# A transformer block on one core: modulation sums in four column groups, square roots kept in written order, and loads moved between queues

## The chip, the cores and the metric

The kernel runs on one core of a Trainium2 chip. The metric is the device time of one execution in microseconds (us). Three executions of the kernel before took 2512.04 us in the median (2508.9 to 2512.86). Besides these there is one profiled execution, whose records all readings below come from.

The engines are named as in the profile: PE is TensorE (PEld its weight loads), DVE is VectorE, ACT is ScalarE, POOL is GpSimd, SP is SyncE, which here does nothing but issue transfers. ACT and POOL can issue transfers too.

## The reference

The input x has two sequences (B = 2) of T = 2048 tokens with D = 512 features; there is one condition vector of 512 values for each sequence. Everything is float32.

```python
mod = silu(condition) @ Wada + bada                    # 6 rows of 512 for each sequence
sh_a, sc_a, gt_a, sh_m, sc_m, gt_m = jnp.split(mod, 6, axis=1)
xm = layernorm(x, g1, be1) * (1.0 + sc_a) + sh_a
x = x + gt_a * attention(xm, Wqkv, Wproj, bproj)       # causal, 16 heads of 32
xm = layernorm(x, g2, be2) * (1.0 + sc_m) + sh_m
h = gelu(xm @ W1 + b1)                                  # 2048 hidden features
x = x + gt_m * (h @ W2 + b2)
```

## The kernel before

The kernel goes through five kinds of stage, the first three once for each sequence.

**Start.** Rows of small parameters (condition, g1, be1, g2, be2, b1) are loaded into the tile `rows` by ACT's queue, turned into columns by one transpose (`ps_c`, copied to `cols`), and silu of the condition goes into `sc`. `modulation(s0)` computes two of the six modulation rows at once: eight products of `sc` (128 rows, 32 columns) with 512 columns of `Wada`, which add up into two groups of 32 partitions of the bank `ps_mod`. DVE adds the bias rows (`mr` or `modr`, loaded from `bada` by ACT's queue), and, where the row is needed as columns, four transposes (`ps_modt`) and a copy follow. It runs three times: at the start, inside group 1 of the first sequence, and inside group 2.

**QKV** (class `Qkv`, L745 ff.). A sequence is cut into four groups (g = 0 to 3) of 512 tokens. `group(g)` makes eight chunks, n = 0 to 7, of queries and keys (`ps_qk`; four products each), then four of values (`ps_v`). Each chunk of queries or keys is split into a high and a low part in a tile `hl`, of which there are two: ACT writes the high half (L797), DVE the low half (L798), and SP stores the tile to memory (L803). The next chunk but one can be written only when that store has landed. After chunk 1, SP also issues the loads of the first keys and queries (`load_keys`, `load_queries`), which wait for the stores before them.

The layernorm of the *next* group is written inside the present one: `between(5)` calls `norm(g + 1, 0)`, and `between(8)` calls `norm(g + 1, 1)`. The first takes the statistics of four tiles of x on DVE, one square root for the four tiles on ACT and a reciprocal on DVE (`inv_std`, L207 to L209), scales the tiles on DVE (`xn`, L229), transposes two of them on PE (`ps_xt`, eight transposes), and applies scale and shift (`xmT`, L248 on DVE and L253 on ACT).

**Order.** A framework schedules the instructions of each engine and may move them against the order in which they are written, by a cost model of its own, except those that pass through `tc.keep_in_program_order`: all of PE's work (`mm`, `transpose`), and what is wrapped in `act(...)`. In the kernel before, the square root of `inv_std` and the copies `hl` are not wrapped, so the scheduler places them on ACT as it sees fit. Each engine then works through its own list from the front; a waiting instruction holds up those behind it.

**Attention** for all 16 heads, 16 units of work; its last act is to store the last unit's row sums (`sum`, L619).

**Projection** (`project_phase`, L913). 16 tiles of tokens, n = 0 to 15, each four products `ps_o`, to which DVE adds the residual (L968) and of which it takes statistics. POOL adds the bias row to the residual first (L961). DVE also multiplies the next quarter's attention output by the inverse row sums (L974). The last unit's sums come back in at n = 0 (`load_sums`, L949, the transfer `r<-sum`), are inverted at n = 3 (L329) and spread at n = 4. During the first sequence's projection the second sequence's QKV weights (`wqkv`, three transfers of 1 MB) are loaded, written at `between(6)`, on ACT's queue; its first layernorm runs at n = 5 and n = 8.

**MLP**, for both sequences together, with seven products in place of eight for each pair of blocks.

Of the kernel before, what the change touches and what calls it, by code (L numbers as in the profile page):

```python
# [8 lines left out]
F32 = mybir.dt.float32  # L9
# [18 lines left out]
def dit_block_kernel(  # L28
# [91 lines left out]
        nc.vector.memset(m.bitcast(F32), 0.0)  # L120
        mhl.append(m)

    pick = const.tile([2 * HD, B, P], F32, tag="pick", name="pick")
    for r in (0, HD):
        nc.vector.tensor_copy(
            pick[r : r + HD],
            ident[r : r + HD, r : r + B].unsqueeze(2).to_broadcast([HD, B, P]),
        )


    cols = const.tile([P, 64], F32, tag="cols", name="cols")
    mod = const.tile([P, 6, C, B], F32, tag="mod", name="mod")
    modr = const.tile([2 * HD, D], F32, tag="modr", name="modr")
    nc.gpsimd.memset(modr, 0.0)
    a1 = const.tile([P, C, B], F32, tag="a1", name="a1")
    c1 = const.tile([P, C, B], F32, tag="c1", name="c1")
# [9 lines left out]
    r_g1 = n_cond  # L146
    r_be1, r_g2, r_be2 = r_g1 + C, r_g1 + 2 * C, r_g1 + 3 * C
    r_b1 = r_g1 + 4 * C
    n_rows = r_b1 + FC


    qd = [
# [30 lines left out]
    def col(r, n):  # L183
        return cols[:, r : r + n]
# [5 lines left out]
    def mm(*args, **kw):  # L190

        return tc.keep_in_program_order(nc.tensor.matmul(*args, **kw))  # L192
# [5 lines left out]
    def transpose(dst, src):  # L198
        n = src.shape[0]
        return tc.keep_in_program_order(nc.tensor.transpose(dst, src, ident[:n, :n]))  # L200
# [4 lines left out]
        nc.vector.bn_aggr(mv[:, n, :], st)  # L205

    def inv_std(mv, rstd, lo, hi):  # L207
        nc.scalar.activation(rstd[:, lo:hi], mv[:, lo:hi, 1], AF.Sqrt, bias=eps)
        nc.vector.reciprocal(rstd[:, lo:hi], rstd[:, lo:hi])  # L209

    def rows_of(psum, r, b, tag):

        ps = psum.tile([P, D], F32, tag=tag, name="ps_rows")
        g = slice(r * HD, (r + 1) * HD)
        mm(ps, pick[g, b, :], modr[g, :], start=True, stop=True)
        return ps

    def transposed(pool_, psum, xts, n0, mv, rstd, a, c, b, dst):
# [523 lines left out]
    class Qkv:  # L742
# [15 lines left out]
        def load_w(self, queue):  # L758
            w_v = Wqkv.rearrange("(c p) f -> p c f", p=P)
            for f in range(0, 3 * D, D):  # L760
                queue.dma_start(self.w[:, :, f : f + D], w_v[:, :, f : f + D])

        def norm(self, g, j):

# [154 lines left out]
    def project_phase(row, psum, between):  # L919

        b = row.b
        with pool(f"proj{b}") as pp:
            n = 0
            ats = list(row.at_s)
            rbs = {1: row.rb_s[1], 2: row.old_queries(), 3: row.rb_s[0]}
            rows_x = [b * NT + i * TQ + t for i in last_order for t in range(TQ)]
            xts = list(row.xt_s)  # L930

            def tokens(upto):
                while len(xts) < min(upto, NT):
                    xt = pp.tile([P, D], F32, tag="xt", name="xt", bufs=6)
                    nc.sync.dma_start(xt, x_rows(rows_x[len(xts)]))
                    xts.append(xt)

            tokens(TQ + 6)
            for k, i in enumerate(last_order):
                if k in (0, 1):  # L940

                    at = pp.tile([P, C, QB], F32, tag="at", name="at", bufs=2)
                    nc.sync.dma_start(at, od[b][last_order[k + 2]])
                    ats.append(at)
                at = ats[k]
                for t in range(TQ):

                    if n == 0:
                        row.load_sums(len(units) - 1, len(units))  # L949
                        nc.sync.dma_start(rbs[2], wide_d[b][last_order[2]])  # L950
                        nc.sync.dma_start(
                            rbs[3][:, : C - 1], wide_d[b][last_order[3]][:, : C - 1]
                        )
                    elif n == 3:
                        row.invert(len(units) - 1, len(units))
                    elif n == 4:
                        row.widen(len(units) - 1, rbs[3][:, C - 1, :])

                    tokens(n + 6)
                    nt, xt = rows_x[n], xts[n]  # L960
                    act(nc.gpsimd.tensor_tensor(xt, xt, bgate, ALU.add))  # L961
                    ps = psum.tile([P, D], F32, tag="mm", name="ps_o")
                    for c in range(C):
                        mm(
                            ps, at[:, c, t * P : (t + 1) * P], row.wproj[:, c, :],
                            start=(c == 0), stop=(c == C - 1),
                        )
                    nc.vector.tensor_tensor(xt, ps, xt, ALU.add)  # L968
                    stats(pp, xt, nt, mv2)
                    nc.sync.dma_start(x1d[nt], xt)  # L970
                    if k + 1 < NQ:
                        d = ats[k + 1][:, t, :]
                        act(
                            nc.vector.tensor_tensor(d, d, rbs[k + 1][:, t, :], ALU.mult)  # L974
                        )
                    between(n)
                    n += 1
        inv_std(mv2, rstd2, b * NT, (b + 1) * NT)


    row = Row(0)
    with pool("wada") as wp, pool("qkv0") as qp, pool(
# [3 lines left out]
        for r, n, src in (  # L986
            (0, n_cond, cond.rearrange("b (c p) -> (b c) p", p=P)),
            (r_g1, C, g1.rearrange("(c p) -> c p", p=P)),
            (r_be1, C, be1.rearrange("(c p) -> c p", p=P)),
            (r_g2, C, g2.rearrange("(c p) -> c p", p=P)),  # L990
            (r_be2, C, be2.rearrange("(c p) -> c p", p=P)),
            (r_b1, FC, b1.rearrange("(c p) -> c p", p=P)),
        ):
            nc.scalar.dma_start(rows[r : r + n, :], src)
        wada_v = Wada.rearrange("(c p) f -> p c f", p=P)
# [2 lines left out]
        def load_wada(s0, s1):  # L998
            w = wp.tile([P, 2, C, D], F32, tag="wada", name="wada")
            if s0 % 3 == 2:  # L1000
                mr = modr
            else:
                mr = wp.tile([2 * HD, D], F32, tag="mr", name="mr")
                nc.gpsimd.memset(mr, 0.0)
            for n, s in enumerate((s0, s1)):
                nc.scalar.dma_start(
                    mr[n * HD : n * HD + B, :],
                    bada[s * D : (s + 1) * D].partition_broadcast(B),
                )
            for k in range(C):  # L1010
                for n, s in enumerate((s0, s1)):
                    nc.sync.dma_start(w[:, n, k, :], wada_v[:, k, s * D : (s + 1) * D])
            wada[s0] = w, mr
# [8 lines left out]
        nc.vector.tensor_copy(cols[:, :n_rows], ps_c)  # L1022
        sc = wp.tile([P, C, HD], F32, tag="sc", name="sc")
        nc.vector.memset(sc, 0.0)
        nc.scalar.activation(
            sc[:, :, :B], col(0, n_cond).rearrange("p (b c) -> p c b", c=C), AF.Silu
        )

        def modulation(s0):

            w, mr = wada.pop(s0)
            ps = ps_sp.tile([2 * HD, D], F32, tag="s", name="ps_mod")
            for k in range(C):
                for n in range(2):
                    mm(
                        ps[n * HD : (n + 1) * HD, :], sc[:, k, :], w[:, n, k, :],
                        start=(k == 0), stop=(k == C - 1),  # L1040
                    )
            nc.vector.tensor_tensor(mr, ps, mr, ALU.add)
            if s0 % 3 == 2:
                return
            ps_t = ps_sp.tile([P, C, 2 * HD], F32, tag="s", name="ps_modt")
            for k in range(C):
                transpose(ps_t[:, k, :], mr[:, k * P : (k + 1) * P])
            nc.vector.tensor_copy(
                mod[:, s0 : s0 + 2],
                ps_t.rearrange("p c (s r) -> p s c r", s=2)[:, :, :, :B],  # L1050
            )

        def scale_shift(a, c, r_g, r_be, shift, scale):

# [6 lines left out]
            nc.vector.tensor_tensor(c, c, mod[:, shift], ALU.add)  # L1061

        halves = [qkv.norm(0, j) for j in range(2)]
        modulation(0)
        scale_shift(a1, c1, r_g1, r_be1, 0, 1)
        for modulate in halves:
# [31 lines left out]
    with pool("qkv1") as qp, pool("ps_qkv1", bufs=6, space=PSUM) as ps_mm:  # L1098
# [2 lines left out]

        def between(n):
            if n == 6:
                qkv.load_w(nc.scalar)
            if n in (5, 8):
                qkv.norm(0, n // 8)()

# [21 lines left out]
    with ExitStack() as mlp:  # L1129
# [38 lines left out]
            return w  # L1168


        vec = wp.tile([B + 1, D], F32, tag="vec", name="vec")
        gb = wp.tile([P, C, B + 1], F32, tag="gb", name="gb")
        gbias = wp.tile([P, C, B], F32, tag="gbias", name="gbias")

        def gate_columns():
            ps = ps_op.tile([P, C, B + 1], F32, tag="o", name="ps_g")
            for k in range(C):
                transpose(ps[:, k, :], vec[:, k * P : (k + 1) * P])
            nc.vector.tensor_copy(gb, ps)
            nc.vector.tensor_tensor(  # L1180
                gbias, gb[:, :, :B], gb[:, :, B:].to_broadcast([P, C, B]), ALU.mult
            )

        def between(n):
            if n == 0:
                nc.vector.tensor_copy(vec[:B], modr[HD : HD + B])
                nc.sync.dma_start(vec[B:], b2.unsqueeze(0))
            if n == 4:
                gate_columns()
            if n in (5, 7):  # L1190
# [283 lines left out]
```

## Time and profile before

| | |
|---|---|
| time, median of 3 | 2512.04 us (2508.9 to 2512.86) |
| profiled execution, time | 2510.99 us |
| its span, first to last instruction | 2509.3 us |
| PE busy | 2440.3 us, 97% of the span |
| DVE busy | 1401.8 us, 56% |
| POOL busy | 978.7 us, 39% |
| ACT busy | 892.6 us, 36% |
| mean TensorE clock granted | 0.990 |

The profiled execution took 2510.99 us, of which 2509.3 us lie between its first and its last instruction. A row of the order in time reads: start in us, length in us, engine, line, operation, output<-input, sizes, count, and in brackets how long the engine sat idle before it and what it then waited for. A matrix product of float32 appears as two records, a transpose as one. "PEclk" in a table of stretches is the share of full clock that TensorE was granted.

### The profile page before, as it was taken

Reading aid. Unit: us, or ns where it says so; the run is one execution under the profiler, and the core shown is the slowest. Engines: PE = TensorE matmul, PEld = TensorE weight load, DVE = VectorE, ACT = ScalarE, POOL = GpSimd, SP = SyncE. Lnnn points to the kernel's source line nnn. Section 1 sums busy time; section 2 is a strip of 40 time slices with the busy share of each in tenths; the row PEclk is TensorE's granted clock in tenths of the full one; section 3 lists DMA queues with packets and bytes.
Section 4 is the critical chain, followed back from the end, with each engine's and each line's share of the span. In section 5 each row is a group of like instructions: output and inputs, shape, how many; then the busy total and the mean of one; then the engine's idle time right before and its main releaser. Section 6 shows DMA issues by size and latency. Waiting matters only on the chain.

```text
span 2509.3 us, 30950 instructions
## 1 busy us (share of the span) xinstructions
PE 2440.3 (97%) x10977; PEld 1178.9 (47%) x10977; DVE 1401.8 (56%) x2820; ACT 892.6 (36%) x1667; POOL 978.7 (39%) x1158
## 2 busy tenths in 40 slices
PE   7999999999999999999999999999999999999998
PEld 3445545445444444554554454444444444444443
DVE  3455667767666535567676766664363353344424
ACT  1213555554545012155545454613313312311310
POOL 0052786766762361068667675332101101200200
PEclk9999999999999999999999999999999999999999
DMA  6667123051224695440514113263224233332423
GB/s 223 202 218 202 46 50 87 22 110 43 87 88 144 215 302 193 133 95 22 110 43 110 27 51 118 69 226 114 88 92 140 78 101 109 109 96 70 140 84 96
DMA packets 133445, 285.71 MB, mean 114 GB/s; under 512 B 13301, under 2 KB 42525, under 8 KB 128426
## 3 DMA queue, kind: packets, MB, share of 16 engines
q1 hardware_dynamic: 126226, 257.47, 34.4%
q0 software_dynamic: 5376, 23.07, 2.6%
q10 hardware_dynamic: 1688, 3.19, 0.4%
q8 instruction: 86, 1.41, 0.2%
q14 instruction: 69, 0.57, 0.1%
HBM read 209.76 MB, written 81.79 MB: 116 GB/s over the span
## 4 chain that ended last, share of the span: by engine, by line
PE 62%; DVE 3%; DMA 1%; SPq 1%; issue 1%; ACT 0%; DVEq 0%; ACTq 0%
PE ps_h L192 15%; PE ps_y L192 15%; PE st L192 9%; PE o L192 5%; PE s L192 5%; PE ps_qk L192 4%; PE ps_o L192 3%; PE sm L192 2%; PE ps_v L192 2%; SPq L336 1%; PE ps_xt L200 1%; PE ps_o L200 0%; DMA r<-sum 0%; DMA q<-hl 0%; DVE junk L436 0%
## 5 line engine op out<-in xcount | busy, mean ns | idle before, releaser
L565 ACT ACTIVATE e<-st 128x512 f32<-128x512 f32 (+1 forms) x1152 | 572.8, 579 | 516.7 <-PE st L192 458.0
L441 DVE TENSOR_REDUCE mx<-s 128x1 f32<-128x512 f32 x634 | 429.6, 687 | 236.2 <-PE s L192 233.4
L593 POOL TENSOR_TENSOR ee<-e 128x512 f32<-128x512 f32 x336 | 420.2, 1287 | 242.8 <-ACT e L565 242.8
L192 PE MATMUL s<-kst,qst 128*128 128x512 f32 (+3 forms) x1066 | 483.4, 460 | 28.4 <-DVE mx L441 10.4
L192 PE MATMUL st<-qst,kst 128*128 128x512 f32 (+3 forms) x1280 | 405.3, 393 | 0.0
L192 PE MATMUL o<-e,vv 128*32 128x512 f32 (+3 forms) x2560 | 296.5, 545 | 0.0
L192 PEld LDWEIGHTS s<-kst,qst 128*128 128x128 f32 x1066 | 201.3, 190 | 202.3 <-DVE mx L441 80.4
L192 PE MATMUL ps_h<-sx,w 128*128 128x512 f32 x640 | 286.7, 592 | 0.0
L1245 POOL TENSOR_TENSOR c<-c 128x512 f32<-128x512 f32 x32 | 40.6, 1270 | 626.8 <-DVE c L1207 626.8
L436 DVE CUSTOM_DVE_ANT_0 junk<-s,causal 128x384 bf16<-128x384 f32 (+3 forms) x432 | 212.2, 491 | 126.9 <-PE s L192 118.2
L192 PE MATMUL ps_y<-sh,w 128*128 128x512 f32 x640 | 276.7, 592 | 0.0
L192 PEld LDWEIGHTS st<-qst,kst 128*128 128x128 f32 x1280 | 226.9, 193 | 92.8 <-issue 63.2
L192 PE MATMUL ps_qk<-xmT,wqkv 128*128 128x512 f32 x512 | 242.0, 601 | 2.2 <-DVE xmT L248 2.2
L571 POOL TENSOR_SCALAR_AFFINE_SELECT e<-e 128x128 f32<-128x128 f32 (+1 forms) x384 | 122.8, 344 | 290.2 <-ACT e L565 284.2
L1207 DVE TENSOR_TENSOR h<-c,ps_h 128x512 f32<-128x512 f32 x128 | 88.0, 688 | 232.5 <-PE ps_h L192 232.5
L593 POOL TENSOR_TENSOR ee<-ee 128x512 f32<-128x512 f32 x168 | 211.2, 1285 | 0.0
L192 PEld LDWEIGHTS ps_h<-sx,w 128*128 128x128 f32 x640 | 121.1, 190 | 150.2 <-issue 149.7
L192 PEld LDWEIGHTS ps_y<-sh,w 128*128 128x128 f32 x640 | 120.7, 190 | 147.8 <-issue 146.4
L1231 ACT ACTIVATE h<-h,cols 128x512 f32<-128x512 f32 x128 | 92.3, 721 | 182.4 <-DVE h L1207 182.4
L192 PE MATMUL st<-fold,sel 32*128 32x512 f32 (+1 forms) x1152 | 154.0, 485 | 2.3 <-DVE fold L500 2.0
L192 PEld LDWEIGHTS ps_qk<-xmT,wqkv 128*128 128x128 f32 x512 | 95.2, 192 | 98.7 <-issue 91.2
L192 PEld LDWEIGHTS st<-fold,sel 32*128 32x128 f32 x1152 | 61.2, 183 | 145.3 <-ACT e L565 75.2
(123 smaller groups left out, 2361.8 us busy)
## 6 DMA issues: line engine op xcount, KB each, us to landing
qst<-q SPq DMA_DIRECT2D x128, 256.0 KB
w<-w1d SPq DMA_DIRECT2D x34, 896.0 KB
w<-w2d SPq DMA_DIRECT2D x28, 1024.0 KB
kst<-k SPq DMA_DIRECT2D x24, 1024.0 KB
q<-hl SPq DMA_DIRECT2D x32, 512.0 KB
k<-hl SPq DMA_DIRECT2D x32, 512.0 KB
kst<-k SPq DMA_DIRECT2D x32, 256.0 KB
w<-in_L_cond_W_dram POOLq DMA_DIRECT2D x64, 128.0 KB, 4.3
```

The lines of the kernel that those rows point to most:

```text
L192: return tc.keep_in_program_order(nc.tensor.matmul(*args, **kw))
L200: return tc.keep_in_program_order(nc.tensor.transpose(dst, src, ident[:n, :n]))
L336: nc.sync.dma_start(dst, inv_d[self.b][u].unsqueeze(1).to_broadcast([HC, HD, QB]),)
L436: nc.vector.tensor_tensor_reduce(junk[:, :w], s[:, :w], causal[:, QB - w :], 1.0, MASKED, ALU.add, ALU.max, m,)
L441: nc.vector.tensor_reduce(m, s[:, :w], axis=AX.X, op=ALU.max)
L565: act(nc.scalar.activation(e[:, :w], sts[h][:, :w], AF.Exp))
L571: nc.gpsimd.affine_select(d, d, pattern=[[0, len(tiles)], [1, P]], compare_op=ALU.is_ge, fill=0.0, base=0, channel_multiplier=-1,)
L593: act(engine.tensor_tensor(dst, x, y, ALU.add))
L1207: nc.vector.tensor_tensor(dst, x, y, op)
L1231: nc.scalar.activation(d, d, AF.Gelu, bias=col(r_b1 + chunk, 1))
L1245: nc.gpsimd.tensor_tensor(c1_, c1_, c2_, ALU.subtract)
```

## The change

1. `modulation`: the eight products go to four groups of 32 partitions, the first and the second half of the inner sum apart; `modr` and `mr` have 128 partitions. The four transposes become four products with `pickc`, a constant of 128 x 4 that picks and adds the halves. `pick` (for `rows_of`) becomes 128 x 2 x 2 x 128.
2. A first square root of a constant at the start, kept in written order.
3. `inv_std`: the square root is wrapped in `act`, and so is the silu.
4. The `bada` rows are loaded by GpSimd's queue.
5. `b2` becomes four more rows of `rows`; `gate_columns` takes the gate straight from `modr` with `pickc`, and the tile `vec` with its copy and its load is gone.
6. `load_w` is wrapped in `act`, and for the second sequence it is issued by GpSimd.
7. The load of the last unit's sums is issued before the residual tiles of the projection.

```diff
+    pickc = const.tile([P, 2, B], F32, tag="pickc", name="pickc")
+    pick = const.tile([P, 2, B, P], F32, tag="pick", name="pick")
+
+    def picks():
+        two = ident.rearrange("p (k r b) -> p k r b", k=2, r=2)[:, :, :, :B]
+        nc.vector.tensor_tensor(pickc, two[:, 0], two[:, 1], ALU.add)
+        nc.vector.tensor_copy(pick, pickc.unsqueeze(3).to_broadcast([P, 2, B, P]))
+
+    first_sqrt = const.tile([P, 1], F32, tag="first", name="first")
+    tc.keep_in_program_order(nc.scalar.activation(first_sqrt, eps, AF.Sqrt))
...
     def inv_std(mv, rstd, lo, hi):
-        nc.scalar.activation(rstd[:, lo:hi], mv[:, lo:hi, 1], AF.Sqrt, bias=eps)
+        act(nc.scalar.activation(rstd[:, lo:hi], mv[:, lo:hi, 1], AF.Sqrt, bias=eps))
         nc.vector.reciprocal(rstd[:, lo:hi], rstd[:, lo:hi])
...
             for f in range(0, 3 * D, D):
-                queue.dma_start(self.w[:, :, f : f + D], w_v[:, :, f : f + D])
+                act(queue.dma_start(self.w[:, :, f : f + D], w_v[:, :, f : f + D]))
...
+            row.load_sums(len(units) - 1, len(units))
             tokens(TQ + 6)
...
                     if n == 0:
-                        row.load_sums(len(units) - 1, len(units))
...
+            (r_b2, C, b2.rearrange("(c p) -> c p", p=P)),
...
-                mr = wp.tile([2 * HD, D], F32, tag="mr", name="mr")
+                mr = wp.tile([P, D], F32, tag="mr", name="mr")
                 nc.gpsimd.memset(mr, 0.0)
             for n, s in enumerate((s0, s1)):
-                nc.scalar.dma_start(
+                nc.gpsimd.dma_start(
...
-            ps = ps_sp.tile([2 * HD, D], F32, tag="s", name="ps_mod")
-            for k in range(C):
-                for n in range(2):
-                    mm(
-                        ps[n * HD : (n + 1) * HD, :], sc[:, k, :], w[:, n, k, :],
-                        start=(k == 0), stop=(k == C - 1),
-                    )
+            ps = ps_sp.tile([P, D], F32, tag="s", name="ps_mod")
+            for k in range(C // 2):
+                for half in range(2):
+                    for n in range(2):
+                        at = (2 * half + n) * HD
+                        kk = half * C // 2 + k
+                        mm(
+                            ps[at : at + HD, :], sc[:, kk, :], w[:, n, kk, :],
+                            start=(k == 0), stop=(k == C // 2 - 1),
+                        )
...
             for k in range(C):
-                transpose(ps_t[:, k, :], mr[:, k * P : (k + 1) * P])
+                mm(
+                    ps_t[:, k], mr[:, k * P : (k + 1) * P], pickc,
+                    start=True, stop=True,
+                )
...
         halves = [qkv.norm(0, j) for j in range(2)]
+        act(
+            nc.scalar.activation(
+                sc[:, :, :B], col(0, n_cond).rearrange("p (b c) -> p c b", c=C), AF.Silu
+            )
+        )
+        picks()
         modulation(0)
...
             if n == 6:
-                qkv.load_w(nc.scalar)
+                qkv.load_w(nc.gpsimd)
...
-                transpose(ps[:, k, :], vec[:, k * P : (k + 1) * P])
+                mm(
+                    ps[:, k], modr[:, k * P : (k + 1) * P], pickc[:, 1],
+                    start=True, stop=True,
+                )
...
         def between(n):
-            if n == 0:
-                nc.vector.tensor_copy(vec[:B], modr[HD : HD + B])
-                nc.sync.dma_start(vec[B:], b2.unsqueeze(0))
```

More of the change, by code (lines that the diff above doesn't have):

```diff
@@ L121, in dit_block_kernel @@
         mhl.append(m)
[L123 to L127, printed above, removed]
-        )
+    pickc = const.tile([P, 2, B], F32, tag="pickc", name="pickc")
[6 more added lines that the diff above has]
+    tc.keep_in_program_order(nc.scalar.activation(first_sqrt, eps, AF.Sqrt))
     cols = const.tile([P, 64], F32, tag="cols", name="cols")
     mod = const.tile([P, 6, C, B], F32, tag="mod", name="mod")
-    modr = const.tile([2 * HD, D], F32, tag="modr", name="modr")
+    modr = const.tile([P, D], F32, tag="modr", name="modr")
     nc.gpsimd.memset(modr, 0.0)
@@ L148, in dit_block_kernel @@
     r_b1 = r_g1 + 4 * C
-    n_rows = r_b1 + FC
+    r_b2 = r_b1 + FC
+    n_rows = r_b2 + C
     qd = [
@@ L213, in rows_of @@
         ps = psum.tile([P, D], F32, tag=tag, name="ps_rows")
-        g = slice(r * HD, (r + 1) * HD)
-        mm(ps, pick[g, b, :], modr[g, :], start=True, stop=True)
+        mm(ps, pick[:, r, b, :], modr, start=True, stop=True)
         return ps
@@ L1024, in dit_block_kernel @@
         nc.vector.memset(sc, 0.0)
-        nc.scalar.activation(
-            sc[:, :, :B], col(0, n_cond).rearrange("p (b c) -> p c b", c=C), AF.Silu
-        )
         def modulation(s0):
             w, mr = wada.pop(s0)
-            ps = ps_sp.tile([2 * HD, D], F32, tag="s", name="ps_mod")
-            for k in range(C):
-                for n in range(2):
-                    mm(
-                        ps[n * HD : (n + 1) * HD, :], sc[:, k, :], w[:, n, k, :],
-                        start=(k == 0), stop=(k == C - 1),
-                    )
+            ps = ps_sp.tile([P, D], F32, tag="s", name="ps_mod")
[8 more added lines that the diff above has]
+                        )
             nc.vector.tensor_tensor(mr, ps, mr, ALU.add)
@@ L1044, in modulation @@
                 return
-            ps_t = ps_sp.tile([P, C, 2 * HD], F32, tag="s", name="ps_modt")
+            ps_t = ps_sp.tile([P, C, 2, B], F32, tag="s", name="ps_modt")
             for k in range(C):
-                transpose(ps_t[:, k, :], mr[:, k * P : (k + 1) * P])
[L1048 to L1051, printed above, removed]
+                mm(
+                    ps_t[:, k], mr[:, k * P : (k + 1) * P], pickc,
+                    start=True, stop=True,
+                )
+            nc.vector.tensor_copy(mod[:, s0 : s0 + 2], ps_t.rearrange("p c s b -> p s c b"))
         def scale_shift(a, c, r_g, r_be, shift, scale):
@@ L1168, in load_w2 @@
             return w
-        vec = wp.tile([B + 1, D], F32, tag="vec", name="vec")
-        gb = wp.tile([P, C, B + 1], F32, tag="gb", name="gb")
+        gb = wp.tile([P, C, B], F32, tag="gb", name="gb")
         gbias = wp.tile([P, C, B], F32, tag="gbias", name="gbias")
         def gate_columns():
-            ps = ps_op.tile([P, C, B + 1], F32, tag="o", name="ps_g")
+            ps = ps_op.tile([P, C, B], F32, tag="o", name="ps_g")
             for k in range(C):
-                transpose(ps[:, k, :], vec[:, k * P : (k + 1) * P])
+                mm(
+                    ps[:, k], modr[:, k * P : (k + 1) * P], pickc[:, 1],
+                    start=True, stop=True,
+                )
             nc.vector.tensor_copy(gb, ps)
             nc.vector.tensor_tensor(
-                gbias, gb[:, :, :B], gb[:, :, B:].to_broadcast([P, C, B]), ALU.mult
+                gbias, gb, col(r_b2, C).unsqueeze(2).to_broadcast([P, C, B]), ALU.mult
             )
         def between(n):
-            if n == 0:
-                nc.vector.tensor_copy(vec[:B], modr[HD : HD + B])
-                nc.sync.dma_start(vec[B:], b2.unsqueeze(0))
             if n == 4:
```

## The prediction, made before the result was known

> **What bounds the kernel.** I first read the page's busy times:
>
> ```profile
> PE 2440.3 (97%) x10977; PEld 1178.9 (47%) x10977; DVE 1401.8 (56%) x2820; ACT 892.6 (36%) x1667; POOL 978.7 (39%) x1158
> ```
>
> PE idles 69 us of 2509.3, so almost any idle time added to PE is added to the end, and an edit off PE is worth only what PE waited for. The next view, PE's waits, says where those 69 us lie. Outside attention the large ones are the start and one stall in the first projection. PE in order of time (start, length, output, records, idle before):
>
> ```profile
> 14.66 3.63 PE L192 MATMUL ps_mod<-wada,sc 128*32 128x512 f32 x16
> ...
> 21.86 23.94 PE L192 MATMUL ps_qk<-xmT,wqkv 128*128 128x512 f32 x48 [2.23 <-DVE xmT L248]
> 45.63 1.04 PE L200 MATMUL ps_xt<-ident,xn 128*128 128x128 f32 x8
> ...
> 801.94 16.57 PE L192 MATMUL ps_o<-kst 128*128 128x512 f32 x38
> 823.25 6.25 PE L192 MATMUL ps_o<-kst 128*128 128x512 f32 x10 [4.74 <-DVE kst L974]
> ```
>
> In the third row the next group's transposes begin with no idle time after chunk 5. In all six QKV groups that prepare a next one it is so. Why, ACT's order of time shows:
>
> ```profile
> 28.67 0.60 ACT L797 ACTIVATE hl<-ps_qk 128x512 fp32r<-128x512 f32 x1 [5.80 <-PE ps_qk L192]
> 29.28 1.28 ACT L208 ACT_TABLE_LOAD   x1
> 30.58 0.30 ACT L208 ACTIVATE rstd<-mv,eps 128x4 f32<-128x4 f32 x1
> 32.10 0.60 ACT L797 ACTIVATE hl<-ps_qk 128x512 fp32r<-128x512 f32 x1 [1.23 <-PE ps_qk L192]
> ```
>
> The table load and the square root stand behind chunk 0's copy, 15 us before PE needs their product. The stall at 818.5 has its cause in DVE's list, and its aftermath in the clock (stretch, PE, PEld, DVE, ACT, POOL busy, PEclk):
>
> ```profile
> 820.00 0.25 DVE L329 RECIPROCAL r<-r 128x16 f32<-128x16 f32 x1 [3.85 <-DMA r<-sum]
> ```
>
> ```profile
> 818.50:823.20 4.70, 0.02 (x1) 0.00 (x0) 3.13 (x7) 0.00 (x0) 1.22 (x2) 1.00 1.03 328
> 823.20:825.00 1.80, 1.75 (x2) 0.74 (x3) 0.00 (x0) 0.00 (x0) 0.00 (x0) 0.55 0.98 360
> 825.00:827.00 2.00, 2.00 (x4) 0.90 (x3) 1.60 (x4) 0.00 (x0) 0.00 (x0) 0.55 0.73 283
> ```
>
> DVE waits for the sums with L974, which PE needs, queued behind. Then PE runs 3.8 us at 0.55 of its clock: 1.7 us more.
>
> **What the Trainium skill says.** "TensorE: Matmul & The Clock Gate", Part 1, says that TensorE falls to half clock after an idle window of about 3.4 us and needs as much activity to come back. The trace agrees: half clock after idles of 4.74 us and 3.20 us (from 717.7 for about 6 us) and after the start's gap (0.50 from 21.8 to 28.0), none after idles near 1 us. "PSUM — Partial Sum Buffer", section on engine and sequencer instructions, says that ScalarE's and VectorE's queues are strictly first in, first out, and that matrix products start in program order. The 3.85 us above agree. "TensorEngine Tiling (Array Packing)", Theoretical Speedup, gives up to 4x for 32 columns. Here `o<-e` with 32 columns takes 1.04 us for 8 records, and `ps_mod` in two groups 3.63 us for 16.
>
> **The change part by part**, against the profiled execution. PE's written order is fixed; what moves are ACT's, DVE's, SP's and POOL's lists, and I read them from the built program.
>
> *Modulation in four groups.* 16 records in fours instead of pairs: 4 rounds of 0.43 us instead of 8, 1.7 us less. That three times is 5.1. The four transposes (0.47 us, one weight load of 0.14 each) become products of two passes, at 0.47 / 4 = 0.12 a pass 8 x 0.12 = 0.95: plus 0.5, twice on the path. No row shows a 4-column product; bounds are 0 and 1.0 (8 x 0.19, a float32 load's length, less 0.47). Net gain 4.1.
>
> *Table ahead, picks.* The table load at the start (1.28) leaves the path, but DVE's reciprocal now stands behind the copy `pick` (512 columns, about 0.55 from 0.27 for 256), which stands behind `cols`, which waits for one more small load. Gain between 0 and 0.5; I take 0.3. The bias rows by GpSimd are needed first at 16 us and cost nothing: POOL is idle there, its transfers of 128 KB land in 4.3 us, and they issue near 3 us.
>
> *Sums first.* The load then waits only for the store of the sums (issued 802.82), so it lands near 808 and DVE no longer waits. What remains is DVE's own work; the second projection, where DVE has no such wait, stalls 1.06 us at the same place. Gain 3.7, plus 1.7 of clock. The six residual tiles queue behind it on SP for about 2 us. POOL had them at 811.5 and PE needs the first at 823, so that is covered. A second wait (1.02 at 855.56) came from DVE waiting 2.39 us for x of group 2, whose statistics the new order moves out of the projection: 1.0. Together 6.4; bounds 4 and 7.5.
>
> *Weights by GpSimd, written at n = 6.* Behind seven adds on POOL, so near 813 instead of 802. Three issues at 0.7 to 1 us hold the add for n = 7 to about 819; PE needs it near 830. The weights are wanted at 867, 45 us later; the 3 MB move at 350 GB/s in 9. Nothing. *b2 rows, no `vec`:* one copy (0.80) and one small load off queues that don't bound: 0.2.
>
> Gains: 4.1 + 0.3 + 6.4 + 0.2 = 11.0.
>
> *Square roots in written order.* This is the cost. They are written after chunk 5, so on ACT they now stand behind the copies of chunks 0 to 5, and on DVE the reciprocal and `xn` behind six low halves. PE's next instructions are the transposes of `xn`: they can't begin before chunk 5 has left PE and been copied. From the end of chunk 5 (0): ACT's copy starts 0.22 later (copies are 3.44 apart, so chunk 5's would start at 45.85 against PE's 45.63) and takes 0.60; DVE's low half 0.69, during which the square root (0.30) runs; reciprocal 0.18; `xn` 0.55; four hand-overs near 0.04. That is 2.3 us of idle PE where there was none, because nothing else is queued on PE that could go first. Four boundaries have just this (groups 1 and 2 of each sequence): 9.2.
>
> At group 0 two things come on top. In the first sequence the table load (1.28) stands before the square root again, since silu came between: 3.1 in place of 2.3. And chunk 5's copy needs the tile whose store (chunk 3) must have landed. SP before:
>
> ```profile
> 33.45 0.38 SPq L803 DMA_DIRECT2D k<-hl  x1
> ...
> 36.98 1.73 SPq L301 DMA_DIRECT2D kst<-k  x4
> 38.75 1.44 SPq L310 DMA_DIRECT2D qst<-q  x3
> 40.28 0.39 SPq L803 DMA_DIRECT2D q<-hl  x1
> 40.99 0.36 SPq L1012 DMA_DIRECT2D wada<-in_L_cond_Wada_dram  x1
> 42.11 0.63 SPq L803 DMA_DIRECT2D k<-hl  x1
> ```
>
> The store of chunk 3 goes at 42.11 and takes 3.5 us to land (chunk 1's: 33.45 to 36.9). In the new order four `wada` loads stand before it instead of one, each waiting for a `kst` load to land, so near 44.5: landing 2.4 to 3.7 us after PE is through with chunk 5. Before, nobody noticed: chunk 4's copy stood at 62.86. Stall 5.3 to 6.6, taken as 6.0. In the second sequence that store goes at 886.66, PE is through at 887.6, and landing takes 3.5 to 5.4: stall 4.6 to 6.5, taken as 5.0. Group 1 there may wait another 0.8. Both long stalls pass the length after which the clock fell; each costs 1.7 to 3, say 2.2. Losses: 9.2 + 6.0 + 5.0 + 0.8 + 4.4 = 25.4.
>
> Sum: 25.4 - 11.0 = 14.4. The profiled span goes from 2509.3 to 2523.7, its time from 2510.99 to 2525.4. The median of the runs lies 1.05 above that execution: **2526.5 us**, 0.6% slower. A measurement of this kernel tells about 0.2% (5 us) from no change.
>
> **Rivals.** *A, nearly no change:* the stores land in time and the clock stays up. Then the losses are 3.1 + 5 x 2.3 = 14.6 against 11: plus 3.6, 2515.6. For it: the landings are estimates, and silence in this trace. Against: SP's own waits for `kst` above. *B, faster:* the chain at the boundaries is short, because ACT's copy and the square root run while PE still drains. Break-even is 11.0 / 6 = 1.8 us a boundary; at 0.8 it is 4.8 against 11.0, minus 6.2, 2505.8. Against: the copy, the reciprocal and `xn` alone are 1.33 us of dependent work after PE's end, so it needs the gain in the projection larger too. *C, slower still:* every boundary drops the clock, also those of 2.3 us: four more times 2.2, plus 8.8, 2535. For it: the start's gap of 2.2 us, with little work before it, ended at half clock. Against: there are 3.4 us of full work around these. *D, the weights come late* (POOL's list blocked until a late residual tile): nothing until they are 45 us late, then one for one; 2532 if by 5 us.
>
> **Numbers.** My case 0.66, A 0.13, B 0.05, C 0.13, D 0.03. My case alone spans 2519 to 2533 (6 us of unsure landings, 4 of clock, 3 of gains). The 8 in 10 reaches into A and C: 2515 to 2536. Slower by over 0.2% (above 2517.1): all of my case, C and D, a quarter of A: 0.85. Within: 0.10. Faster: 0.05.
>
> **What would show it.** Right: PE idle before the transposes of the next group in six places, released by `xn`, near 2.3 us in four and 4 to 7 in the two groups 0; PEclk near 0.5 after these two; ACT's square root right behind the sixth copy; `ps_mod` near 1.9 us for 16 records; the stall at 818.5 down to about 1. Wrong: no idle time at the six places, or long copies waiting for stores in groups 1 and 2 as well, or PE waiting for `wqkv` at the second sequence's start.

## The result and the profile after

Measured: 2573.57 us in the median of 4 runs (2568.81 to 2575.77), against 2511.18 for the kernel before on the same chip. The ratio is 1.0247 (95% interval 1.0229 to 1.0264): 2.5% slower, where 0.6% was forecast. The profiled execution has a span of 2570.3 us, 61.0 more than before.

Busy times, from the page of the kernel after:

```profile
PE 2451.6 (95%) x10989; PEld 1187.2 (46%) x10989; DVE 1421.2 (55%) x2819; ACT 894.6 (35%) x1668; POOL 986.1 (38%) x1167
```

PE is busy 11.3 us longer and idle for 118.7 us in place of 69.0. So 49.7 of the 61.0 us are idle PE. Where it idles, PE's waits say (sum, number, longest, in us):

```profile
PE ps_xt L207 <- DVE xn L235: 51.8, 9, 15.3
...
PE ps_o L199 <- DVE at L980: 5.5, 3, 3.9
...
PE ps_o L199 <- DVE kst L980: 2.7, 2, 1.6
```

Before, the first of these rows had 3.1 us in two waits. PE in order of time, with the two sets of modulation products first and the transposes of the next group after them:

```profile
13.41 2.56 PE L199 MATMUL ps_mod<-wada,sc 128*32 128x512 f32 x16
...
20.21 4.64 PE L199 MATMUL ps_qk<-xmT,wqkv 128*128 128x512 f32 x5 [2.23 <-DVE xmT L254]
...
54.39 2.21 PE L207 MATMUL ps_xt<-ident,xn 128*128 128x128 f32 x8 [10.96 <-DVE xn L235]
...
93.69 1.92 PE L199 MATMUL ps_mod<-wada,sc 128*32 128x512 f32 x16
...
107.73 2.21 PE L207 MATMUL ps_xt<-ident,xn 128*128 128x128 f32 x8 [4.65 <-DVE xn L235]
...
930.66 2.21 PE L207 MATMUL ps_xt<-ident,xn 128*128 128x128 f32 x8 [15.26 <-DVE xn L235]
...
989.71 2.21 PE L207 MATMUL ps_xt<-ident,xn 128*128 128x128 f32 x8 [11.93 <-DVE xn L235]
...
1043.31 1.44 PE L207 MATMUL ps_xt<-ident,xn 128*128 128x128 f32 x8 [2.92 <-DVE xn L235]
```

With the boundary of group 2 in the first sequence (2.83 and 1.71 in two pieces) the six places hold 50.3 us of idle PE, where 21.0 were forecast. The third row answers the one of before at 45.63, which had no idle time. What stretched it is read from ACT's order of time:

```profile
36.60 0.60 ACT L803 ACTIVATE hl<-ps_qk 128x512 fp32r<-128x512 f32 x1 [2.84 <-PE ps_qk L199]
47.40 0.60 ACT L803 ACTIVATE hl<-ps_qk 128x512 fp32r<-128x512 f32 x1 [10.20 <-DMA q<-hl]
51.33 0.60 ACT L803 ACTIVATE hl<-ps_qk 128x512 fp32r<-128x512 f32 x1 [3.34 <-DMA k<-hl]
51.95 1.28 ACT L215 ACT_TABLE_LOAD   x1
53.24 0.30 ACT L215 ACTIVATE rstd<-mv,eps 128x4 f32<-128x4 f32 x1
```

These are the copies of chunks 3, 4 and 5, the table load and the square root. Chunk 4's copy waits 10.2 us for the store of chunk 2, then chunk 5's copy another 3.34 for the store of chunk 3, and the square root is behind both. The same time on SP:

```profile
31.08 0.38 SPq L809 DMA_DIRECT2D k<-hl  x1
31.56 0.41 SPq L316 DMA_DIRECT2D qst<-q  x1
34.64 2.88 SPq L307 DMA_DIRECT2D kst<-k  x4
37.56 1.38 SPq L316 DMA_DIRECT2D qst<-q  x3
39.04 0.38 SPq L809 DMA_DIRECT2D q<-hl  x1
39.47 3.81 SPq L1019 DMA_DIRECT2D wada<-in_L_cond_Wada_dram  x4
44.04 0.38 SPq L809 DMA_DIRECT2D k<-hl  x1
```

The store of chunk 2 (512 KB) is issued at 39.04, behind four loads `kst` and four loads `qst` of 256 KB each, 2 MB in all. It has landed when chunk 4's copy starts, at 47.4: 8.4 us. At the other long boundaries the same store takes 9.2 us (94.95 to 104.1), 14.4 (912.40 to 926.85) and 10.7 (975.42 to 986.1). The store of chunk 3, issued after it, is the one that lands last, and so ends the wait: it takes 7.3 us here (44.04 to 51.33), and 10.2, 15.5 and 11.3 at the other three. The longest of these, in the second sequence, on SP and ACT:

```profile
913.08 0.69 SPq L809 DMA_DIRECT2D k<-hl  x1
```

```profile
928.62 0.60 ACT L803 ACTIVATE hl<-ps_qk 128x512 fp32r<-128x512 f32 x1 [1.17 <-DMA k<-hl]
```

The stores also start late. Chunk 2's tile is complete at 34.5, but SP stands before the loads `kst` and `qst`, whose own waits come first in its list, and issues the store at 39.04. The clock follows the idle time, as forecast (stretch and columns as in the prediction):

```profile
48.00:54.30 6.30, 0.00 (x0) 0.00 (x0) 2.07 (x5) 2.18 (x3) 0.00 (x0) 0.50 0.88 300
54.40:58.00 3.60, 3.60 (x10) 2.39 (x11) 2.39 (x5) 1.10 (x2) 0.00 (x0) 0.50 0.82 227
```

Cut into stages, the two traces compare as follows. The first three rows are of before: QKV of the first sequence from its first product to attention, the first projection, QKV of the second sequence. (The row of the projection ends with its last product, 0.16 us after the first of QKV. Counted to the first product of QKV, as below, it took 64.9.)

```profile
21.86:225.76 203.90, 201.37 (x564) 97.06 (x565) 102.33 (x239) 36.21 (x66) 41.59 (x60) 0.98 0.63 201
...
801.94:866.99 65.05, 59.29 (x149) 26.50 (x146) 41.57 (x91) 4.99 (x9) 19.80 (x17) 0.97 0.71 239
866.99:1060.74 193.75, 190.79 (x528) 93.75 (x528) 95.99 (x218) 34.02 (x62) 60.32 (x96) 1.00 0.65 210
```

The same three of after:

```profile
20.21:245.88 225.67, 204.51 (x568) 100.29 (x569) 103.06 (x239) 37.15 (x66) 41.31 (x60) 0.94 0.57 184
...
826.08:894.64 68.56, 60.58 (x148) 27.17 (x145) 42.13 (x81) 4.69 (x8) 22.34 (x20) 0.95 0.61 215
894.64:1120.08 225.44, 195.15 (x530) 96.75 (x528) 97.31 (x228) 34.98 (x63) 60.25 (x96) 0.93 0.57 184
```

The start is 1.65 us shorter, QKV 21.8 and 31.5 us longer, the first projection 3.7 longer. Attention is 4.0 and 2.5 longer, the second projection and the MLP 0.4 and 0.5 shorter. The sum is 61.0. The projection, where 6.4 us were to be won, lost. Its stall at 818.5 did shrink, to 1.61 and 1.10 us, but two new ones came (PE and DVE in order of time):

```profile
843.41 1.13 PE L199 MATMUL ps_o<-kst 128*128 128x512 f32 x2 [1.61 <-DVE kst L980]
845.64 4.56 PE L199 MATMUL ps_o<-kst 128*128 128x512 f32 x10 [1.10 <-DVE kst L980]
...
863.57 1.13 PE L199 MATMUL ps_o<-kst,at 128*128 128x512 f32 x2 [3.91 <-DVE at L980]
866.05 2.08 PE L199 MATMUL ps_o<-kst,at 128*128 128x512 f32 x2 [1.36 <-DVE at L980]
```

```profile
853.81 0.69 DVE L211 BATCH_NORM_STATS2 stat<-x 128x6 f32<-128x512 f32 x1 [4.73 <-DMA x<-in_x_dram]
```

DVE waits for x of the next sequence, with the products `at` that PE needs behind it.

### The profile page after: what moved, and what is told of

Same layout as the page of the kernel before. It is cut to its first block, busy times and chain, and to the rows that moved or that the text cites. A ratio compares the mean times of both kernels' runs of the same rounds, so it can differ in the third digit from the quotient of the medians.

```text
span 2570.3 us, 30988 instructions
## 1 busy us (share of the span) xinstructions
PE 2451.6 (95%) x10989; PEld 1187.2 (46%) x10989; DVE 1421.2 (55%) x2819; ACT 894.6 (35%) x1668; POOL 986.1 (38%) x1167
## 5 line engine op out<-in xcount | busy, mean ns | idle before, releaser
L199 PE MATMUL ps_qk<-xmT,wqkv 128*128 128x512 f32 x512 | 248.7, 615 | 2.2 <-DVE xmT L254 2.2
```

## The experiments

Theory 1: nearly all of the loss is the square root's place. It stands behind the copies of chunks 0 to 5, and the copies of chunks 4 and 5 stand behind stores that are slow to land because 2 MB of loads go ahead of them (theory 1a; its rival 1b lays this to `wada` and other traffic). Rival 2: the other edits carry the loss. Rival 3: the dependent work after chunk 5 is long by itself.

**One edit undone.** The kernel after, with the square root free again.

```diff
-        act(nc.scalar.activation(rstd[:, lo:hi], mv[:, lo:hi, 1], AF.Sqrt, bias=eps))
+        nc.scalar.activation(rstd[:, lo:hi], mv[:, lo:hi, 1], AF.Sqrt, bias=eps)
```

> The kernel after, with only the square root of inv_std placed freely again; on ACT it then stands behind the copies of chunks 0 to 2 instead of 0 to 5. Theory 1 (the square root's place, with the stores it must outwait, cost nearly everything: 50.3 us of idle PE at six boundaries and some 12 to 20 us of clock, partly the same time): the six waits for xn vanish and the time falls to 2509 to 2520 us. Rival 2 (the projection's late loads, the weights by GpSimd and the start carry the loss): above 2545 us.

Measured: 2513.56 us, ratio to before 1.0001 (0.9987 to 1.0016). In its order of time on ACT the table load and square root stand behind chunk 0's copy again; on PE the transposes follow chunk 5 at once.

```profile
25.36 0.60 ACT L803 ACTIVATE hl<-ps_qk 128x512 fp32r<-128x512 f32 x1 [4.36 <-PE ps_qk L199]
25.97 1.28 ACT L215 ACT_TABLE_LOAD   x1
28.18 0.30 ACT L215 ACTIVATE rstd<-mv,eps 128x4 f32<-128x4 f32 x1 [0.93 <-DVE mv L212]
```

```profile
35.45 7.03 PE L199 MATMUL ps_qk<-xmT,wqkv 128*128 128x512 f32 x16
42.32 1.04 PE L207 MATMUL ps_xt<-ident,xn 128*128 128x128 f32 x8
```

SP issues chunk 2's store at 39.13 here, as late as in the kernel after (39.04). It holds up no PE work, because the square root that PE's next products need is already done. Theory 1 stands; rival 2 asked for over 2545.

**The same edit alone.** The kernel before, with only the square root kept in written order.

```diff
-        nc.scalar.activation(rstd[:, lo:hi], mv[:, lo:hi, 1], AF.Sqrt, bias=eps)
+        act(nc.scalar.activation(rstd[:, lo:hi], mv[:, lo:hi, 1], AF.Sqrt, bias=eps))
```

> The kernel before, with only the square root of inv_std kept in written order. Theory 1: the loss comes with this one edit, so the time rises by 45 to 60 us, to 2555 to 2572, with six PE waits for xn of some 50 us together. Rival 2 (it needs the other edits, for example four loads of wada on SP in front of the stores in place of one): the waits are 2.3 to 6 us each, together 20 to 25 us, and the time is 2531 to 2540.

Measured: 2569.58 us, ratio 1.0216 (1.0187 to 1.0245). From PE's waits:

```profile
PE ps_xt L200 <- DVE xn L229: 52.2, 9, 14.8
```

The loss needs no other edit. Its make-up is not quite the same as in the kernel after. Of the 52.2 us, 7.4 lie at the start, and the six boundaries hold 44.7 in place of 50.3; group 0 of the first sequence stalls 7.17 us in place of 10.96, with no table load there and no `wada` between the two stores. At the start PE's first transposes wait 7.24 us for `xn`, because silu with its table load, and then the square root's table load, stand ahead of the first square root on ACT. The first product of QKV starts at 28.2 us in place of 21.9. The change, which places silu behind that square root, has no such wait.

**Stores out of the way.** The kernel after with four tiles `hl`, so that chunks 4 and 5 need the stores of chunks 0 and 1.

```diff
-                    hl = hp.tile([P, 2, MT], F32R, tag="hl", name="hl", bufs=2)
+                    hl = hp.tile([P, 2, MT], F32R, tag="hl", name="hl", bufs=4)
```

> The kernel after, with four tiles hl in place of two, so that chunk 4's and chunk 5's copies need the stores of chunks 0 and 1 and not of 2 and 3. Theory 1 (the boundaries are long because chunk 4's copy waits for chunk 2's store): each of the six waits falls to the chain of dependent work alone, 2.3 us (3 at the first), together about 15, and the clock holds there; 35 to 50 us faster than the kernel after, 2522 to 2538. Rival 3 (the chain itself, or ACT and DVE behind in their work, makes the boundaries long): less than 10 us faster than the kernel after.

Measured: 2526.82 us, ratio 1.0049 (1.0034 to 1.0063). PE's waits:

```profile
PE ps_xt L207 <- DVE xn L235: 15.9, 9, 3.1
```

The six boundaries hold 3.09, 2.08, 2.27, 2.08, 2.18 and 2.05 us, 13.8 together. The copies ahead of the square root wait for no store here. So this is the price of the written order itself; the rest of the 50.3, some 36.5 us, was waiting for stores. Rival 3 falls.

**What the stores wait for.** The kernel after, with the first keys and queries loaded behind the stores of all eight chunks. These loads and the stores are also wrapped in `act`, so that SP keeps the written order; the cut below leaves that out.

```diff
-                if f == 0:
+                if f == 3:
```

> The kernel after, with the loads of the first keys and queries issued behind the stores of all eight chunks (two feature rows later), in written order on SP. Theory 1a (chunk 2's store lands 8 to 14 us after its issue because the loads kst and qst stand in the transfer queues ahead of it): the stores land within 3 to 5 us, the six waits for xn come to 15 to 25 us together instead of 50, and the time is 2530 to 2550. Rival 1b (the traffic of wada and of other transfers, or the store itself, makes the landing long): landings stay at 8 us or more and the time above 2560.

Measured: 2555.07 us in two runs, ratio 1.0159 (1.0113 to 1.0205). In this order of time on SP, chunk 2's store goes at 33.91, and chunk 4's copy starts at 39.43 with no wait for it, so it has landed within 5.5 us:

```profile
33.91 0.38 SPq L809 DMA_DIRECT2D q<-hl  x1
34.33 0.47 SPq L1019 DMA_DIRECT2D wada<-in_L_cond_Wada_dram  x1
34.84 0.79 SPq L393 DMA_DIRECT2D bgate<-in_L_cond_bproj_dram  x1
37.34 0.38 SPq L809 DMA_DIRECT2D k<-hl  x1
```

In the second sequence, with no `wada` about in either kernel, chunk 3's store goes at 909.91 and chunk 5's copy starts at 915.42 without waiting for it: 5.5 us at most, where 15.5 were needed. So theory 1a holds and 1b falls. The stores gain twice, since they are also issued as soon as their tile is complete. PE's waits:

```profile
PE ps_xt L207 <- DVE xn L235: 16.8, 9, 3.1
PE s L199 <- DMA qst<-q: 15.1, 2, 9.3
```

The waits for `xn` fell as theory 1a expected, from 51.8 to 16.8. The time did not fall as far: 2555 against the 2530 to 2550 expected, because the loads that had been in the way now come late, and PE waits for them once in each sequence (9.26 and 5.86 us). So these loads may not simply be moved back.

**The projection.** With the square root free, the first projection was still 68.1 us long, against 64.9 before. Theory P: GpSimd issues the weights' 3 MB some 10 us later than ACT did, and they collide with small transfers on the sums' way. The next version gives the weights back to ACT, in free order, and was also meant as the best of both kernels.

```diff
-        act(nc.scalar.activation(rstd[:, lo:hi], mv[:, lo:hi, 1], AF.Sqrt, bias=eps))
+        nc.scalar.activation(rstd[:, lo:hi], mv[:, lo:hi, 1], AF.Sqrt, bias=eps)
...
-                act(queue.dma_start(self.w[:, :, f : f + D], w_v[:, :, f : f + D]))
+                queue.dma_start(self.w[:, :, f : f + D], w_v[:, :, f : f + D])
...
-                qkv.load_w(nc.gpsimd)
+                qkv.load_w(nc.scalar)
```

> The kernel after, with the square root of inv_std placed freely and the second sequence's weights loaded by ACT, placed freely, both as in the kernel before. With the square root alone made free, QKV of the first sequence was 5.2 us shorter than before and the first projection 3.2 us longer (68.1 against 64.9). Theory P (the projection's forecast gain was eaten by the weights' 3 MB, which GpSimd issues 11 us later, beside the loads of x and the inverse sums): the first projection falls to 58 to 61 us and the time to 2500 to 2506, 0.2 to 0.45% under the kernel before. Rival Q (issuing the sums first moves the other transfers badly by itself): the projection stays at 66 to 69 and the time at 2507 to 2513.

Measured: 2507.35 us, ratio 0.9981 (0.9968 to 0.9994), so a little faster than before, and clearly faster than after. The projection took 65.4 us: shorter than 68.1, but not the 58 to 61 expected. Next come the two edits, each alone on the kernel before. First the sums:

```diff
+            row.load_sums(len(units) - 1, len(units))
             tokens(TQ + 6)
...
-                        row.load_sums(len(units) - 1, len(units))
```

> The kernel before, with only the load of the last sums issued ahead of the residual tiles. Theory P: the stall of 4.7 us in the first projection falls to 1 to 2.7, no new wait of 3 us comes, the projection takes 58.5 to 61 us in place of 64.9, and the time is 4 to 6 us lower than before. Rival Q: the projection is not shorter than 64, with a new wait of DVE for x or of PE for at.

Measured: 2509.45 us, ratio 0.9996 (0.9986 to 1.0006), projection 65.2 us. The stall fell from 4.74 to 2.63, and PE waited 0.85 and 2.34 for `at` instead. DVE waited 2.61 for x. On PE:

```profile
818.62 4.56 PE L192 MATMUL ps_o<-kst 128*128 128x512 f32 x10 [2.63 <-DVE kst L974]
833.49 1.12 PE L192 MATMUL ps_o<-kst,at 128*128 128x512 f32 x2 [0.85 <-DVE at L974]
836.95 1.31 PE L192 MATMUL ps_o<-kst,at 128*128 128x512 f32 x2 [2.34 <-DVE at L974]
```

Why the stall fell only to 2.63 can be read from DVE. Two `xn` stand between the inverse of the sums and the product `kst` that PE waits for. Here they run while GpSimd adds the bias rows, and take 2.73 us; before, with the sums later, GpSimd had just finished (at 819.7), and they took 0.91:

```profile
813.71 2.73 DVE L229 TENSOR_SCALAR xn<-qst,mv,rstd 128x512 f32<-128x512 f32 x2
```

```profile
820.17 0.91 DVE L229 TENSOR_SCALAR xn<-qst,mv,rstd 128x512 f32<-128x512 f32 x2
```

By an estimate from these rows, 1.8 of the 2.63 us are this. In the other versions with the sums first, too, two of the three `xn` there take some 2.7 us or more together, and with the weights alone 4.29. No run takes GpSimd's additions away, so that they are the cause is not tested.

And the weights alone:

```diff
-                queue.dma_start(self.w[:, :, f : f + D], w_v[:, :, f : f + D])
+                act(queue.dma_start(self.w[:, :, f : f + D], w_v[:, :, f : f + D]))
...
-                qkv.load_w(nc.scalar)
+                qkv.load_w(nc.gpsimd)
```

> The kernel before, with only load_w changed: kept in written order and, for the second sequence, issued by GpSimd, so about 11 us later. Theory P: the 3 MB collide with the loads behind them, and the first projection grows from 64.9 to 68 to 72 us, 3 to 7 us in the time. Rival Q (as forecast, it costs nothing): the projection stays at 64 to 66.

Measured: 2512.67 us, ratio 1.0006 (0.9994 to 1.0017), projection 65.1 us. Alone, this edit costs nothing, as the prediction had it, and theory P is wrong about it. Only both together lengthen the projection: 67.7 to 68.6 us in the five traces that have both with the weights at n = 6, against 65.1 to 65.4 in the three so far that have one of them. Then the weights were issued later still, in the version with the free square root, at n = 10 and at n = 9:

```diff
-            if n == 6:
+            if n == 10:
```

> The kernel after with the square root placed freely, and the second sequence's weights issued by GpSimd at n = 10 of the projection in place of n = 6, so some 15 to 20 us later, when the inverse sums have been loaded back. Theory P (the 3 MB delay whichever small transfer of the sums' way is under way: the store of the sums, 5.6 us where ACT issued the weights first against 1.7 where they came later; inv 7 to 9 us where they came beside it against 2.0 in the second projection): both take 1.7 to 3 us, the waits of DVE for x and of PE for at shrink to under 1 us each, the projection falls from 68.1 to 59 to 63 us, and the time is 0.25 to 0.5% under the kernel before (2498 to 2506). Rival Q (the projection is held by the order on SP, not by the weights): 65 us or more. Rival R (the weights come late for the second sequence): PE waits for wqkv when the projection has ended.

> The same with n = 9, where GpSimd issues the 3 MB after its tenth addition and not its eleventh, about when inv is issued. Theory P: inv takes 7 us or more to land, with the waits behind it, and the projection stays at 66 to 70 us. Rival Q: no difference from n = 10.

Measured: 2517.93 us (ratio 1.0018, 1.0008 to 1.0027) and 2518.06 us (1.0017, 1.0007 to 1.0027). The projection took 71.4 us in both. In the first, `inv` still takes 5.8 us (815.21 to 821.05), though the weights go out only at 830.07. Then it is a residual tile and x that land late, and PE waits 5.32 us for `at`. So theory P, that the weights only have to be clear of the sums' way, falls. At n = 9 it expected 66 to 70 us; what came, no difference from n = 10, is what its rival expected. A last pair, with the square root free in both, has the final spread of the inverse sums (`qst<-inv`) issued by ACT, so that SP doesn't stand waiting for `inv` with the loads of x behind it; the first with the weights on ACT, the second with them on GpSimd at n = 6:

```diff
-            nc.sync.dma_start(
-                dst,
-                inv_d[self.b][u].unsqueeze(1).to_broadcast([HC, HD, QB]),
-            )
+            src = inv_d[self.b][u].unsqueeze(1).to_broadcast([HC, HD, QB])
+            if dst is None:
+                nc.sync.dma_start(wide_d[self.b][i][:, c, :], src)
+            else:
+                act(nc.scalar.dma_start(dst, src))
```

> The kernel after with the square root placed freely and the weights on ACT placed freely, and in addition the last spread of the inverse sums (the transfer qst<-inv) issued by ACT in place of SP, so that SP doesn't stand still while inv lands. Theory S (the gain forecast for the projection is lost on SP: the spread waits 7 us for inv with the loads of x behind it, so DVE's statistics and the products at behind them come late): DVE's waits for x and PE's for at shrink, the projection falls from 65.4 to 60 to 63.5, and the time is 0.25 to 0.45% under the kernel before. Rival U (the landing of inv and of the loads under the 3 MB is the limit, whoever issues): the projection stays at 64.5 to 67.

> The same spread by ACT, but with the weights by GpSimd at n = 6 as in the kernel after (square root free). Theory S: the projection falls from 68.1 to 62 to 65, since DVE no longer waits 4.8 us for x. Rival U: it stays at 67 to 69, with DVE waiting for x, whose loads queue behind the weights in the transfers, or with PE waiting for at since ACT's square root, which needs x, stands before the spread.

Measured: 2513.85 us (ratio 1.0000, 0.9986 to 1.0014) and 2514.01 us (0.9999, 0.9983 to 1.0015), the projection 67.5 and 67.7, for 65.4 and 68.1 without this edit. In the second SP issues x at 820.5 to 826, yet DVE waits 4.64 us for it:

```profile
829.72 0.69 DVE L211 BATCH_NORM_STATS2 stat<-x 128x6 f32<-128x512 f32 x1 [4.64 <-DMA x<-in_x_dram]
```

Theory S falls too: here an earlier issue doesn't make the loads land in time. What is shown is that no placing tried here turned the earlier sums into a shorter projection (65.2 to 71.4 us, against 64.9 before), and that with the sums first a later issue of the weights makes it longer. Which transfer decides in each arrangement stays open.

## Why the prediction was wrong

The direction was right, from the step that was meant to give it; the time of 2526.5 us and the range to 2536 were far too low. By its own terms, against the profiled span (forecast +14.4, measured +61.0):

**Square roots in written order: the path right, the landing of the stores mis-sized.** Rival A put the chain alone at 14.6 us for six boundaries; with the stores out of the way it measures 13.8. (The terms of one chain add up to 2.4, not to the 2.3 that was used; 2.05 to 2.27 came at the five without a table load.) The prediction also had the wait that ends last: chunk 5's copy for chunk 3's store. At group 0 of the first sequence even the moment of issue was close, 44.04 for a forecast of 44.5, though PE was through with chunk 5 at 43.4 and not at 45.6. What failed is the step "landing takes 3.5 to 5.4". It took 7.3 us at group 0 of the first sequence and 15.5 at that of the second. The forecast came from chunk 1's store of before, which was in front of the loads `kst` and `qst`. The stores that matter are behind these, as the SP rows quoted in the prediction show. And the step was asked at group 0 alone. Group 1 issues the same loads, its stores of chunk 3 took 10.2 and 11.3 us, and its two boundaries were given 2.3 and 3.1 us where 4.65 and 11.93 came. The six places hold 50.3 us for a forecast of 21.0: 29.3 of the 46.6 us by which the sum was short. The prediction had named long copies waiting for stores in later groups as what would show it wrong.

**Clock: the kind right, the size not.** Half clock after the long stalls came as said. But it fell after five of the six boundaries rather than two, and after the sixth, with 2.92 us of idle time, it held. Against the version with the free square root, PE is busy 7.3 and 4.5 us longer in the two QKV stages (204.51 for 197.25, 195.15 for 190.68), some 12 us where 4.4 were forecast. Idle time and clock together, the written order costs 25.3 us up to the first attention and 31.5 in the second QKV, some 57 for a forecast of 25.4.

**Modulation, table, start: right in the sum.** Sixteen products take 1.92 us at full clock (forecast 1.9), `ps_modt` 1.05 in place of 0.47 (forecast plus 0.5), and QKV begins 1.65 us earlier, for 1.5 forecast. At the start the parts differ and make up for each other, which is luck: the products begin 1.25 us earlier (13.41 for 14.66) where 0.3 was forecast for table and picks, and they gain 1.07 (2.56 for 3.63) and not 1.7. With the square root free, start and QKV of the first sequence together take 220.0 to 220.8 us in six traces, against 225.8 in the trace of before and 223.9 and 224.3 in two others that leave this stage alone: 3.1 to 5.8 saved, for 4.4 forecast.

**Sums first: wrong.** The step that failed is "DVE no longer waits. What remains is DVE's own work". DVE's wait for the sums went, but it waits for x instead (2.61 us with this edit alone, 4.73 in the kernel after), and its own work before `kst` grew beside GpSimd's additions. Alone the edit won about nothing; in the change the projection became 3.7 us longer, 10.1 off the forecast of minus 6.4. The pattern was the second projection, which takes 60 us; but that one loads neither weights nor the next sequence's x.

**Weights by GpSimd: right alone, wrong with the sums first.** The slack of 45 us until their own use was real: no rival D. Left out was that a later issue of 3 MB changes when the other loads of the stage land; which of them decides is not shown.

The remaining 6.5 us are attention, 4.0 and 2.5. Its first stage scattered between 574.9 and 585.9 us over the traced executions of all these versions, so this is not laid to the change.

Rival C lay nearest in size, but what it named, half clock after every boundary, is the smaller part; most of the loss is idle time.

## What to carry to other kernels

When an instruction moves behind others in an engine's queue, ask of each one ahead of it what *it* waits for, the transfers that free its buffer among them; here a 0.3 us square root inherited the landing times of two stores. A landing time read from a trace holds for a store with the same transfers in front of it: count what is issued before it. Removing one wait pays only up to the next wait on the same path, so look for that one, and for what the work behind it will now run beside, before adding up the gain.

## What was not expected of the hardware

The length of an idle stretch alone doesn't say whether the clock falls. With four tiles `hl`, PEclk was 0.50 for some 3 us after idles of 2.08 (at 93.44), 2.08 (898.58) and 2.18 us (947.03), and 1.00 after 3.09, 2.27 and 2.05 us; in the version with the loads behind the stores it was 0.50 after 3.09 us. The Trainium skill, "TensorE: Matmul & The Clock Gate", Part 1, speaks of an idle window of about 3.4 us; here shorter ones were enough at times. So a part of rival C's mechanism, half clock after idles near 2.3 us, does exist.

Stores of the same 512 KB took from at most 5.5 us to 15.5 us to land, by what had been issued ahead of them. From the issue of the 8 KB `inv` to that of the transfer that reads it, 5.8 to 9.2 us passed in the first projection with the sums loaded first, the 5.8 with the weights not yet issued; in the second projection of the version best of both it was 2.05. One DVE operation, `xn`, took 2.75 us in the first projection of the kernel after, at 838.93, while GpSimd was adding, and 0.54 at 857.18, with nothing on GpSimd. And the time of one version scattered more than the prediction took for granted: 20 runs of the version with the free square root lay between 2502 and 2526 us, and gave an interval of 0.15% to either side.
